# New due times, an opening set by hand and one multiplication on GpSimd in a four-layer graph-attention kernel whose instruction order a planner writes

## The chip, the cores and the metric

The kernel runs on one core of a Trainium2 chip. The metric is device time in microseconds (us) of one execution. Seven executions of the kernel before took 2975.5 to 2980.1 us, with a median of 2978.17 us. One execution was recorded by the hardware profiler; all rows, groups, waits and timelines below come from it.

The engines are named as in the profile: PE is TensorE (matrix products), PEld its weight load, DVE is VectorE, ACT is ScalarE, POOL is GpSimd, and SP is SyncE, which here only issues transfers. ACT's queue (ACTq) can issue transfers too. "L582" is line 582 of the kernel's source.

## The reference

Sixteen entries of 1024 nodes by 256 features pass through four graph-attention layers, each with a layer norm and a ReLU in front and a residual behind. All entries share one 1024 by 1024 mask, `adj`.

```python
# layer 0 (four heads of 64); layer 3 is the same with another a
h = jnp.maximum(_layernorm(x), 0.0)
Wh = (h @ W).reshape(B, N, 4, 64)
e = s_src[:, :, None, :] + s_dst[:, None, :, :]      # scores: Wh times the vectors a
e = jnp.where(e > 0, e, 0.2 * e)
alpha = softmax(where(mask, e, -inf), axis=2)
x = x + elu(einsum('bijh,bjhd->bihd', alpha, Wh))
# layer 1: one head of 256, scores of the same form
# layer 2: e = (h @ W1) @ (h @ W2).T, values h @ W3, relu in place of elu
```

## The kernel before

**Tiles.** A node set is cut into eight tiles of 128 nodes, and the mask and the attention weights into two halves of 512 query nodes. One weight tile `p` is 128 key nodes by 512 queries. Layers 0 and 3 make 64 such tiles for each entry (two halves, four heads, eight key tiles), layers 1 and 2 make 16 each.

**A layer's steps.** Statistics of x on DVE (L822 and L823). Then the norm's factors in three steps: `norm` (L855, DVE), `norm2` (L858, a power on POOL) and `norm3` (L861, DVE, which gives `nshift`). ACT makes the normed h (L891). h is turned over, either on PE (L906, then the copy L929) or, for nearly all entries, by a transposing DMA from SP (L918, with copies L914 and L932). PE projects it onto W and the score columns (`projected`, through the helper at L582). `evict` (L968 to L977, ACT) takes the exponentials of the scores: `ke` for the factors and the last column of `val`; in some layers `scaled` (L983, DVE) then multiplies the values by that column. The factors are spread to rows of 512: for entry 0 of layer 0 and entry 15 of layer 3 by PE and ACT (L1025 and L1029), otherwise through DRAM (L1047, L1051, L1064). `weigh` makes a weight tile with one DVE instruction (L1117 in layers 0 and 3, L1208 in layer 1). Layer 2 makes its scores on PE, exponentials on ACT (L1235, L1236) and cuts them with two DVE instructions (L1240, L1241). `attend` multiplies the weights with `val` on PE: into `acc` in layers 0 and 3, into `accb` in layers 1 and 2. Last come a reciprocal (L1150 or L1267), a division (L1164 or L1161 into `o`, L1273 or L1275 into `o1`), the ELU (L1083, L1084, L1088) and the addition to x: on DVE (L1090) or, in the layers that are marked `filling` (layer 0, and layer 3 of the last two entries), on POOL (L1097).

**The opening.** SP issues three transfers for x of entry 0 (L636), four quarters of the mask (L729), and then the later weights. ACT issues `w0` (L654) and its vector `a` (L664) and then loads its table with a first exponential (`warm`, L715). The score columns of `w0` are made by scaling `a` (L674), multiplying (L684) and adding up (L697), all on DVE, in two chunks c = 0 and 1. Each mask quarter is compared on DVE (`pos`, L737), turned over on PE (L595) and kept by a copy (L750: DVE for the first half, ACT for the second).

**What sets the order.** `Plan` (L79 on) takes every step with an engine, a cost in us, a due time, the steps it comes after, and the buffers it takes and gives. It plays these forward in the build, always taking the ready step with the earliest due, and writes the instructions in the order found. Nothing of costs and dues remains in the program but this order. At run time an engine waits only on semaphores that follow from data and buffers; a step that is planned "after" another without sharing data with it is kept back only by its place in its queue.

Due times come from tables: `PERIOD` (190 us for an entry), `START` and `LATER` (where a layer of an entry starts), `LEAD`, `AHEAD` and `STEP` (how far ahead its prologue lies, and the spacing in it), `WHEN` (steps of layers 1 and 2) and `EARLY` (how much earlier the ends are due). `SOON` is a due before all others. Buffers of note: eight for `p` (layers 0 and 3), eighteen for `p1`, two for `acc`, one for `o`, four for `pp` (the shared accumulator banks).

Of the kernel before, what the change touches and what calls it, by code (L numbers as in the profile page):

```python
# [45 lines left out]

PERIOD, EARLY = 190.0, 0.7407
START = {0: 0.0, 1: 1.0372, 2: 2.297, 3: 3.5524}  # L50
LEAD = {0: 0.7046, 1: 0.4612, 2: 0.2956, 3: 1.6786}
STEP = {0: 0.01, 1: 0.0686, 2: 0.0892, 3: 0.0445}
WHEN = {
    (1, "weights"): ((-0.5242, 0.0026), (-0.1464, 0.0419)),
    (1, "attended"): ((0.7567, 0.0147), (0.2574, 0.106)),
    (2, "weights"): ((-0.0331, 0.0103), (0.3531, 0.0135)),
    (2, "attended"): ((0.642, 0.0926), (0.4636, 0.0079)),
# [3 lines left out]
    (1, 0): 0.596, (1, 1): 0.958, (13, 2): 0.03, (13, 3): 0.392, (14, 3): -0.089, (0, 2): -0.137, (12, 2): 0.2,  # L61
    (13, 1): -0.61, (13, 0): 0.042, (0, 1): 0.165, (14, 2): 0.012, (12, 3): 0.381, (15, 2): 0.061,
    (14, 1): 0.153, (0, 3): -0.204, (0, 0): 0.005, (15, 1): 0.169, (3, 0): -0.106, (3, 2): -0.226,
    (3, 1): -0.037, (3, 3): 0.253, (14, 0): -0.403, (15, 3): 0.422, (12, 0): 0.216, (2, 2): -0.002,
    (2, 3): -0.052, (12, 1): -0.053, (1, 3): 0.022,
}
AHEAD = {
    (1, 0): 0.818, (15, 3): 0.338, (12, 1): 1.914, (15, 1): 0.404, (1, 3): -1.162, (0, 3): 0.168,
    (14, 2): 0.163, (14, 1): -0.3, (1, 1): -0.058, (0, 2): 0.142, (13, 1): 0.271, (3, 1): 0.197, (14, 3): 0.426,
    (3, 3): -0.404, (2, 2): 1.115, (15, 0): -0.042, (12, 0): 0.12, (1, 2): 0.321, (2, 3): -0.168,  # L70
    (3, 2): -0.354, (2, 1): -0.221, (13, 3): -0.364, (0, 1): 0.057, (12, 3): 0.014, (0, 0): -0.016,
    (13, 2): -0.254,
# [467 lines left out]
def fast(  # L540
# [16 lines left out]
    nc = tc.nc  # L557
# [87 lines left out]
    def weight(w, name, due, a=None, heads=0, own=1):  # L645
# [10 lines left out]
        s = landed(plan.add(engine, 0.5, due, load), due, 256)  # L656
# [12 lines left out]
        s2 = landed(plan.add(engine, 0.5, due, load_a, take=("p1",)), due, own * d)  # L669
# [8 lines left out]
        for c in range(KC):  # L678

            def columns(c=c):  # L680
                wa = tiles["wa", c] = buf("u", [P, heads, 2, d], name="wa")
                for side in range(2):
                    of = tiles["a"][:, :, side, :]
                    (nc.vector if first else nc.gpsimd).tensor_mul(  # L684
# [7 lines left out]
            for hd in range(1 if first else heads):  # L692
# [15 lines left out]
                )  # L708
        return t, done[-1]

    first_x = load_x(0, SOON)

    def warm():

# [113 lines left out]
    class Layer:  # L828
# [7 lines left out]
        def prologue(self, due, step, stats, direct=False):  # L836
# [48 lines left out]
            for n, t0 in enumerate(range(0, NT, 2)):  # L885
# [37 lines left out]
                def kept(t0=t0):  # L923
# [4 lines left out]
                    if direct:  # L928
                        nc.scalar.copy(T["hT", t0], T["tp", t0])  # L929
                        return  # L930
# [544 lines left out]
```

## Time and profile before

The profiled execution took 2980.87 us on the device, of which the instructions span 2979.0 us.

| | PE | DVE | ACT | POOL |
|---|---|---|---|---|
| busy, us | 2914.0 | 2645.3 | 1922.6 | 234.5 |
| share of the span | 98% | 89% | 65% | 8% |

| group | count | busy, us | what it is |
|---|---|---|---|
| PE L582 acc<-val,p | 32768 | 1074.9 | attended values of layers 0 and 3 |
| PE L582 accb<-val,p | 8192 | 928.1 | attended values of layers 1 and 2 |
| PE L582 pp<-qT,hT | 2048 | 461.4 | scores of layer 2 |
| DVE L1117 p<-row,ke,mask | 2048 | 1460.2 | weights of layers 0 and 3 |
| DVE L1208 p<-row,ke,mask | 256 | 180.2 | weights of layer 1 |
| DVE L822 bn<-xt | 512 | 211.9 | statistics |
| POOL L1097 xt<-xt,o | 35 | 97.5 | additions to x on POOL |

A group's row gives line, engine, operation, output<-inputs and count, then busy time and mean ns of one. A timeline row gives start and duration in us, then the same names and a count (of merged instructions), and in brackets the idle time of that engine just before and what ended it. A row of the view by stretches gives, for each engine, the busy time and the number of instructions, then the granted PE clock (1.00 is full), the share of the 16 DMA engines that was busy, and GB/s. One product in the kernel's code can be two rows of the profile (the weights of one `p` give 16 rows of `acc`).

### The profile page before, as it was taken

The numbers are of one execution on the slowest core, as the hardware profiler recorded it, in microseconds if no ns is written. First come the engines' busy times: TensorE is split into PE (matmuls) and PEld (weight loads), VectorE is DVE, ScalarE is ACT, GpSimd is POOL, SyncE is SP. The second block draws the span as 40 slices with busy tenths as digits, with TensorE's granted clock in tenths as the row PEclk, the third lists the DMA queues.
The fourth block names the chain that finished last, engine by engine and source line by source line (L and its number), as shares of the span: only waits on it lengthen the run. The fifth ranks groups of instructions, "written<-read, shape, count | busy, mean of one in ns | idle before, by whom it ended". The sixth has DMA issues, their size and how long they took to land.

```text
span 2979.0 us, 108647 instructions
## 1 busy us (share of the span) xinstructions
PE 2914.0 (98%) x47954; PEld 2326.2 (78%) x47954; DVE 2645.3 (89%) x5286; ACT 1922.6 (65%) x4776; POOL 234.5 (8%) x151
## 2 busy tenths in 40 slices
PE   7799999999999999999999999999999999999997
PEld 5776868779697887878779787786877869796876
DVE  8989988899898899989899898988999999796698
ACT  6767776785656767566675656766656684656543
POOL 2111100000100000000000100000000010000001
PEclk9899999999999999999999999999999999999999
DMA  4432223332222332413233222231413332121210
GB/s 126 94 59 59 64 50 97 63 69 73 44 71 61 70 72 61 79 38 87 48 66 77 48 77 44 72 75 38 90 42 70 76 62 57 41 57 35 53 35 25
DMA packets 344049, 188.06 MB, mean 63 GB/s; under 512 B 268881, under 2 KB 304401, under 8 KB 343569
## 3 DMA queue, kind: packets, MB, share of 16 engines
q1 hardware_dynamic: 343152, 180.51, 27.0%
q8 instruction: 378, 6.19, 0.9%
q14 instruction: 103, 0.84, 0.1%
q10 hardware_dynamic: 416, 0.52, 0.1%
HBM read 98.63 MB, written 17.33 MB: 39 GB/s over the span
## 4 chain that ended last, share of the span: by engine, by line
PE 84%; DVE 13%; ACT 1%; issue 1%; DMA 0%; POOL 0%; SPq 0%; DVEq 0%; POOLq 0%
PE pp L582 31%; PE accb L582 27%; PE acc L582 26%; DVE p L1117 8%; DVE o L1088 1%; DVE bn L822 1%; DVE xt L1090 0%; DVE p L1241 0%; DVE mv L823 0%; DVE p L1240 0%; DMA xt<-in_x_dram 0%; ACT hTp L932 0%; POOL xt L1097 0%; DMA turned<-planes 0%; DVE rden L1150 0%
## 5 line engine op out<-in xcount | busy, mean ns | idle before, releaser
L1117 DVE SCALAR_TENSOR_TENSOR p<-row,ke,mask 128x512 f32<-128x512 f32 x2048 | 1460.2, 767 | 34.0 <-PE acc L582 32.7
L582 PEld LDWEIGHTS acc<-val,p 128*64 128x64 f32 x32768 | 1073.0, 139 | 121.0 <-issue 47.2
L582 PE MATMUL acc<-val,p 128*64 128x65 f32 x32768 | 1074.9, 223 | 38.9 <-DVE p L1117 33.8
L582 PE MATMUL accb<-val,p 128*64 128x257 f32 x8192 | 928.1, 380 | 0.0
L582 PEld LDWEIGHTS accb<-val,p 128*64 128x64 f32 x8192 | 736.0, 136 | 130.1 <-issue 4.1
L582 PE MATMUL pp<-qT,hT 128*64 128x512 f32 x2048 | 461.4, 592 | 0.0
L582 PE MATMUL pp<-w,hTp 128*64 128x264 f32 (+1 forms) x3072 | 382.9, 387 | 3.0 <-ACT hTp L932 2.0
L582 PEld LDWEIGHTS pp<-qT,hT 128*64 128x64 f32 x2048 | 171.4, 137 | 211.6 <-issue 209.0
L582 PEld LDWEIGHTS pp<-w,hTp 128*64 128x64 f32 x3072 | 245.1, 138 | 84.4 <-issue 14.1
L891 ACT ACTIVATE h<-xt,nshift,rstd 128x256 f32<-128x256 f32 x512 | 275.5, 596 | 38.3 <-DVE nshift L861 38.2
L1240 DVE SCALAR_TENSOR_TENSOR p<-u,p 128x512 f32<-128x512 f32 x256 | 175.7, 686 | 127.8 <-ACT p L1236 127.5
L1275 ACT ACTIVATE o<-accb,rdens 128x256 f32<-128x256 f32 x128 | 60.5, 473 | 347.3 <-DVE rdens L1267 340.8
L914 ACT COPY planes<-h 128x512 uint16<-128x512 uint16 x496 | 281.7, 621 | 0.0
L932 ACT COPY hTp<-turned 128x1024 uint16<-128x1024 uint16 x184 | 214.0, 1167 | 28.5 <-DMA turned<-planes 28.3
L822 DVE BATCH_NORM_STATS2 bn<-xt 128x6 f32<-128x256 f32 x512 | 211.9, 414 | 13.4 <-DMA xt<-in_x_dram 5.4
L1235 ACT ACTIVATE u<-pp 128x512 f32<-128x512 f32 x256 | 152.9, 597 | 104.7 <-PE pp L582 79.3
L1164 ACT ACTIVATE o<-acc,rden 128x64 f32<-128x64 f32 x572 | 132.2, 316 | 113.3 <-DVE rden L1150 99.8
L858 POOL TENSOR_TENSOR rstd<-rstd,neg_half 128x8 f32<-128x8 f32 (+2 forms) x67 | 124.5, 1858 | 975.9 <-DVE rstd L855 643.2
L1241 DVE TENSOR_TENSOR p<-p,mask 128x512 f32<-128x512 f32 x256 | 179.2, 700 | 8.8
L1097 POOL TENSOR_TENSOR xt<-xt,o 128x1024 f32<-128x1024 f32 x35 | 97.5, 2786 | 1131.7 <-DVE o L1088 980.3
L1208 DVE SCALAR_TENSOR_TENSOR p<-row,ke,mask 128x512 f32<-128x512 f32 x256 | 180.2, 738 | 0.5 <-DMA row<-er_d 0.5
L977 ACT ACTIVATE val<-pp,val 128x64 f32<-128x64 f32 (+1 forms) x640 | 179.5, 347 | 0.0
(87 smaller groups left out, 1911.9 us busy)
## 6 DMA issues: line engine op xcount, KB each, us to landing
row<-er_d SPq DMA_DIRECT2D x272, 256.0 KB, 3.4
xt<-in_x_dram SPq DMA_DIRECT2D x31, 512.0 KB, 5.2
out_dram<-xt SPq DMA_DIRECT2D x31, 512.0 KB, 3.6
raw<-in_adj_dram SPq DMA_DIRECT2D x4, 1024.0 KB, 15.3
raw<-in_adj_dram SPq DMA_DIRECT2D x16, 256.0 KB, 3.3
turned<-planes SPq DMA_TRANSPOSE x248, 3.1
xt<-in_x_dram SPq DMA_DIRECT2D x2, 256.0 KB
w<-in_L_gnn_W_dram SPq DMA_DIRECT2D x2, 256.0 KB
```

Source lines behind the costliest of these rows:

```text
L582: nc.tensor.matmul(to[c : c + COLS], stationary[:, c : c + COLS], moving, start=start, stop=stop, skip_group_check=True,)
L822: nc.vector.bn_stats(st, x_tiles[b][:, t, :])
L891: nc.scalar.activation(h, x_tiles[b][:, t, :], AF.Relu, bias=T["shift"][:, t : t + 1], scale=T["rstd"][:, t : t + 1],)
L914: nc.scalar.copy(to[:, :, :, k, :], of)
L932: nc.scalar.copy(bits, T["tp", t0].rearrange("p s c q -> p c q s"))
L977: nc.scalar.mul(to[:, hd, :], of[:, hd, :], a[:, hd, :])
L1117: nc.vector.scalar_tensor_tensor(p, lay.rows[half, hd], lay.ke[:, lay.heads + hd, jt : jt + 1], mask_of(half, jt), op0=OP.max, op1=OP.mult)
L1164: nc.scalar.mul(to[:, t, :], acc[:, t, :d], rden[:, t, :])
L1208: nc.vector.scalar_tensor_tensor(p, lay.rows[half, 0], lay.ke[:, 1, jt : jt + 1], mask_of(half, jt), op0=OP.max, op1=OP.mult)
L1235: nc.scalar.activation(u, e, AF.Exp, scale=1.0 - SLOPE)
L1240: nc.vector.scalar_tensor_tensor(p, u, 1.0, p, op0=OP.max, op1=OP.mult)
L1241: nc.vector.tensor_mul(p, p, mask_of(half, jt))
```

## The change

It has six parts.

1. **Tables.** `EARLY`, `START`, `LEAD`, `STEP`, `WHEN`, `LATER` and `AHEAD` have new values, so all entries are ordered anew.
2. **Dues in the opening.** x of entry 0 is due 10 us ahead of `SOON`, `warm` 9, `w0` 6, the mask's first quarter 5.2, its second 1.5, and the norms and the prologue 5. The statistics are spaced by 0.5 in place of 0.9, and the norm steps of all three parts are due together.
3. **Order of loads.** In the plan the mask's loads come after parts of x, and the loads of `w1`, `w2v`, `w3` and the two raw weights of layer 2 after the first mask quarter.
4. **`w0`'s score columns.** The multiplication of chunk c = 1 is issued on POOL in place of DVE and no longer waits for chunk 0.
5. **Rows.** A new list `factored` holds the `evict` steps. The spreading of rows, and the factors that go through DRAM, come after these, no longer after `scaled`. The first half's rows of the two PE-turned layers are due 2.5 steps earlier.
6. **Costs in the plan.** `norm2`, `pos`, `keep` and the multiplication have other cost entries. `TURNED_ON_PE` names the two layers that `direct` named, so the same two turn h on PE.

Both programs have the same instructions but for one: two of the multiplications at L684 are on POOL in place of DVE.

```diff
-PERIOD, EARLY = 190.0, 0.7407
-START = {0: 0.0, 1: 1.0372, 2: 2.297, 3: 3.5524}
-LEAD = {0: 0.7046, 1: 0.4612, 2: 0.2956, 3: 1.6786}
-STEP = {0: 0.01, 1: 0.0686, 2: 0.0892, 3: 0.0445}
+TURNED_ON_PE = ((0, 0), (15, 3))
+PERIOD, EARLY = 190.0, 0.8711
+START = {0: 0.0, 1: 1.0292, 2: 2.3297, 3: 3.7503}
+LEAD = {0: 0.5727, 1: 0.718, 2: 0.2478, 3: 2.1041}
+STEP = {0: 0.0094, 1: 0.0707, 2: 0.069, 3: 0.055}
...
-    (1, 0): 0.596, (1, 1): 0.958, (13, 2): 0.03, (13, 3): 0.392, (14, 3): -0.089, (0, 2): -0.137, (12, 2): 0.2,
...
-    (3, 1): -0.037, (3, 3): 0.253, (14, 0): -0.403, (15, 3): 0.422, (12, 0): 0.216, (2, 2): -0.002,
...
+    (1, 0): 0.176, (1, 1): 0.626, (13, 3): 0.356, (0, 2): -0.59, (12, 3): 0.485, (14, 1): 0.247, (0, 3): -0.2,
...
+    (14, 0): -0.416, (2, 2): -0.232, (2, 0): -0.016, (3, 0): -0.452, (15, 3): -0.422, (3, 3): 0.208,
...
-        s = landed(plan.add(engine, 0.5, due, load), due, 256)
+        begin = () if first else tuple(mask_ready[0, 0])
+        s = landed(plan.add(engine, 0.5, due, load, begin), due, 256)
...
-                    (nc.vector if first else nc.gpsimd).tensor_mul(
+                    (nc.vector if at_once else nc.gpsimd).tensor_mul(
...
-            m = plan.add(*((DVE, 0.7) if first else (POOL, 2.0)), due + 0.5, columns, (s, s2, *done), take=("u",))
+            m = plan.add(
+                *((DVE, 0.7) if first and c == 0 else (POOL, 1.7)), due + 0.5, columns, (s, s2, *(() if first else done)),
+                take=("u",),
+            )
...
-    first_x = load_x(0, SOON)
+    first_x = load_x(0, SOON - 10.0)
...
-    w0, w0_ready = weight(w_l0, "w0", SOON, a_l0, 4, 4)
-    plan.add(ACT, 1.6, SOON, warm)
+    plan.add(ACT, 1.6, SOON - 9.0, warm)
+    w0, w0_ready = weight(w_l0, "w0", SOON - 6.0, a_l0, 4, 4)
...
-            due, quarter = 15.0 + n if half else SOON + n, {}
+            due, quarter = 15.0 + n if half else -1.5 if jh else SOON - 5.2, {}
...
-            loaded = landed(plan.add(SP, 0.9, due, load, take=("x",)), due, 1024)
+            loaded = landed(plan.add(SP, 0.9, due, load, (first_x[2 if n == 0 else -1],), take=("x",)), due, 1024)
...
-                at = due - (len(parts) - n - 1)
+                at = due - 5.0 * (len(parts) > 1)
                 s = plan.add(DVE, 0.2, at, norm, (*stats[its], ready[-1] if n else None))
-                s = plan.add(POOL, 2.0, at, norm2, (s,))
+                s = plan.add(POOL, 0.6 + 0.17 * (its.stop - its.start), at, norm2, (s,))
...
                     s2 = plan.add(ACT, cost, at, evict, (s2,), give=() if many else ("pp",))
+                    factored.append(s2)
...
-                            PE, 0.44, at + (half * heads + hd) * 0.01, spread, tuple(evicted[half * HT : (half + 1) * HT]),
+                            PE, 0.44, at - 2.5 * step * (1 - half) + (half * heads + hd) * 0.01, spread, tuple(factored[half * HT : (half + 1) * HT]),
...
-            due, step = SOON, 0.1
-            stats = [statistics(b, t, due - 2.5 + t // 2 * 0.9, (loads[b][t],)) for t in range(NT)]
+            due, step = SOON - 5.0, 0.1
+            stats = [statistics(b, t, due - 2.5 + t // 2 * 0.5, (loads[b][t],)) for t in range(NT)]
```

## The prediction

> **What bounds the kernel now.** First the slices of the span (40 of 74.5 us) and four stretches of it.
>
> ```profile
> PE   7799999999999999999999999999999999999997
> DVE  8989988899898899989899898988999999796698
> PEclk9899999999999999999999999999999999999999
> ```
>
> ```profile
> 0.00:75.00 75.00, 56.61 (x1040) 43.61 (x1040) 63.58 (x138) 46.46 (x141) 16.38 (x22) 1.00 0.43 127
> 75.00:200.00 125.00, 105.36 (x1986) 92.33 (x1988) 117.78 (x247) 84.37 (x256) 16.81 (x10) 0.89 0.36 74
> 200.00:2900.00 2700.00, 2689.36 (x43530) 2136.16 (x43528) 2399.37 (x4789) 1766.30 (x4303) 189.53 (x117) 1.00 0.28 62
> 2900.00:2979.00 79.00, 62.64 (x1404) 54.10 (x1400) 64.60 (x116) 25.43 (x77) 11.79 (x3) 0.91 0.07 23
> ```
>
> PE is idle for 65.0 us in all: 18.4 up to 75, 19.6 up to 200, 10.6 in the 2700 us that follow, and 16.4 in the tail. The middle is PE at work; a new order can win next to nothing there. In the first 200 us and the last 79, DVE is busy 94% and 82% of the time, and PE waits for it. The waits of PE say so by name:
>
> ```profile
> PE acc L582 <- DVE p L1117: 33.8, 34, 8.3
> PE pp L906 <- ACT h L891: 12.0, 1, 12.0
> PE acc L582 <- ACT o L1164: 3.9, 1, 3.9
> ```
>
> The timeline of the opening shows where DVE itself is late, and one later row what POOL does to it:
>
> ```profile
> 9.55 0.43 DVE L822 BATCH_NORM_STATS2 bn<-xt 128x6 f32<-128x256 f32 x1 [0.23 <-DMA xt<-in_x_dram]
> 11.16 0.13 DVE L861 SCALAR_TENSOR_TENSOR nshift<-mv,rstd 128x2 f32<-128x2 f32 x1
> 18.50 0.15 DVE L861 SCALAR_TENSOR_TENSOR nshift<-mv,rstd 128x4 f32<-128x4 f32 x1
> 19.30 5.25 PE L582 MATMUL pp<-w,hTp 128*64 128x264 f32 x28 [1.02 <-DVE w L697]
> 27.39 4.29 POOL L684 TENSOR_TENSOR wa<-w,a_bc 128x256 f32<-128x256 f32 x4 [11.57 <-DVE a_bc L674]
> 27.76 3.42 DVE L1117 SCALAR_TENSOR_TENSOR p<-row,ke,mask 128x512 f32<-128x512 f32 x3
> ...
> 70.70 2.81 POOL L1097 TENSOR_TENSOR xt<-xt,o 128x1024 f32<-128x1024 f32 x1 [6.47 <-DVE o L1088]
> 71.30 2.76 DVE L1117 SCALAR_TENSOR_TENSOR p<-row,ke,mask 128x512 f32<-128x512 f32 x1
> ```
>
> The first weight starts only at 27.76. A weight takes 0.667 us in a run (4.70 for 7 at 52.20); beside POOL's addition one took 2.76.
>
> **The method.** Both programs hold the same instructions, so I compare instruction orders. I price them by rows: a weight 0.667 on DVE, its product on PE 0.466 (3.73 for 128 rows); a statistics pair 0.53; an `accb` tile 3.48 (17.40 for five); a projection tile 0.88. For a weight, its lag is the DVE work listed up to and with it, less the PE work listed ahead of its product. PE's lost time there is at least that lag plus all that DVE waited or was slowed.
>
> **Opening and fill, before.** The lag is largest at a weight behind 160 weights, 56 statistics pairs and the rest: 106.7 + 29.7 + 11.5 (ELU) + 13.9 (mask, values) + 8.6 (small ones) = 170.4 of DVE. PE has 136.7 ahead: 143 products 66.7, eight `accb` tiles 27.8, 33 projections 29.0, turns 13.2. Lag 33.7. In the trace this product starts at 196.7, so 60.0 was lost, and DVE's own waits and slowdowns are 60.0 - 33.7 = 26.3. Of these, 11.6 lie before the end of the 7th weight (36.75 by the clock, 25.2 of work); 14.7 come after.
>
> **The opening, after.** SP's first twelve loads keep their order; "behind x" is only in the plan, since no wait was added between them. One SP load moves: the second raw weight goes ahead of x of entry 1. It took 0.43 to issue, and that x is first read at 39.48, 18 us after it was issued: nothing, or 0.43 without that cover. On ACT's queue the table load (1.28) and the exponential (0.20) now precede the two `w0` issues, which go from 0.74 to some 2.3. `w0` landed 3.8 after its issue, so 6.1; DVE scales `a` at about 12. Nothing, by that cover; without it, up to 1.6.
>
> On DVE, `nshift` of part 1 comes after the first statistic of part 3 in place of the fourth: 9.55 + 0.61 = 10.1 against 11.16. The third comes at about 14.1 against 18.50, because the scaling (0.4), one multiplication (0.74) and one sum (0.69) are all that is left ahead of it, and the mask's eight steps come behind. POOL's two multiplications (1.09 each, as in the 4.29 above) start at 13.4 and end by 15.6; the second sum follows one mask copy, at 16.7 to 17.4, against 19.26. Six projections of 0.88 then end at 22.7, three spreads and a copy (0.57) later the first row stands, since rows no longer wait for the scaled values: first weight at 24.1. Two comparisons (0.37), four mask copies (0.64) behind PE's turns, two values and six weights later the 7th weight ends at 33.5. Its DVE work is 23.3, so waits are 10.2, 1.4 fewer. If x comes 0.7 sooner, without `w0` beside it, this is 0.7 more; if the `a` vector is late by the 1.6 above, it is gone.
>
> A rule that speaks against moving work to POOL is in the Trainium skill, SBUF — State Buffer, section Who interferes with whom: GpSimd and VectorE share a port pair as an exclusive lock, and a two-input VectorE instruction is fully blocked while GpSimd reads. The row at 71.30 agrees (2.1 us lost). By the rule the third `nshift`, which has two inputs, could be held for 1.09, and the sum below would be 1.1 smaller. The comparison beside POOL at 27.43 took its usual 0.42, and `nshift` comes before or just after POOL starts, so I leave it out.
>
> **The fill, after.** The lag peaks at 32.1 (PE work 100.1) and at 29.6 (PE work 156.6: 166.9 products 77.8, eight `accb` tiles 27.8, 43 projections 37.8, turns 13.2; DVE 186.3). Later waits: I keep the 14.7, and 11.0 to the first place. To them I add 0.6, since `w1`'s two pairs on POOL now stand beside weights alone: four weights at 61.76 beside one pair took 1.0 too long, three at 27.76 beside two pairs 1.4. Lost at the first: 32.1 + 10.2 + 11.6 = 53.9; at the second: 29.6 + 10.2 + 15.3 = 55.1. The second decides: 60.0 - 55.1 = 4.9 gained. Bounds: 0, if DVE's waits grow by what the lag shrinks, to 9, if the later waits are as short as at the first place and x is 0.7 sooner (60.0 - 53.9 + 0.7 = 6.8) and the three waits of DVE for PE's `acc` at 87, 91 and 108 (2.9 in all) go by a third to two thirds.
>
> **The middle.** With eight `p` buffers a weight cannot start before the product eight back is done. Counting DVE and PE work from there, the worst place from 300 on has 0.8 to spare before and 0.7 after: nothing. Bounds: 5.6, PE's stalls on weights from 600 to 2400, gained, to the same lost again, twice.
>
> **The tail.** After the last `accb` tile 79 weights' products remain before, 88 after. DVE's list from the last `accb` reciprocal is 58.2 against 65.0 us: 6.8 more, while PE's work ahead of that tile is 5.9 less. Net 0.9 lost. In the tail one POOL addition met weights and held the only `o` buffer:
>
> ```profile
> 2924.60 7.49 POOL L1097 TENSOR_TENSOR xt<-xt,o 128x1024 f32<-128x1024 f32 x1 [15.17 <-DVE o L1088]
> 2933.11 5.82 PE L582 MATMUL acc<-val,p 128*64 128x65 f32 x112 [3.93 <-ACT o L1164]
> ```
>
> After the change nine weights in place of eight lie in that gap: 0.7 less idle. Together 0.2 lost; from 3.9 gained (POOL at its usual 2.8) to 6.8 lost (PE not sooner at that tile).
>
> **Sum.** -4.9 + 0 + 0.2 = -4.7. The profiled execution took 2980.9 (span 2979.0 and 1.9 around it), 2.7 above the median: 2976.2 by it, and 2973.5 by the median of 2978.2. I call 0.2%, 6 us, what a measurement of this kernel can tell from no change.
>
> **Rivals.** *More falls away*: the first place decides (6.1), and POOL's addition in the tail meets no weights (3.9): 2968. For it: the lag is small where most waits were; against it: both additions stand beside weights in the new list too. *The opening's gain is waited out*: weights come sooner, but `acc` and `p` buffers come free at PE's pace, so DVE waits longer in the fill; part 3 does nothing: 2977. For it: 2.9 us of such waits already; against it: the lag itself shrinks by 4.1. *Slower*: a weight late in the repeating middle. The spare there is 0.7; the longest such stall in the middle was 1.2, and with DVE or ACT late by that much at one place in each of some 13 repeats PE loses 15.6: 2978 - 4.7 + 15.6 = 2989. It decides against me once PE's waits from 300 to 2700 exceed 15 us, where the stretches before give 8.9. For it: every due is new; against it: both orders have the same spare.
>
> **Numbers.** The forecast, 2970 to 2976, has 0.45; a third of it is over 6 us faster. More falls away 0.27; waited out 0.13; slower 0.15 (0.13 beyond 6 us). Faster 0.15 + 0.27 = 0.42, same 0.30 + 0.13 + 0.02 = 0.45, slower 0.13. The range goes from below the faster rival, for its own error, to part of the slow one: 2964 to 2982.
>
> **What would show it.** First weight at 24 and the 7th done by 34; PE idle under 17 up to 75 and its waits for weights down by some 5; the first mask copy beside POOL's multiplications; 18 us idle or less in the tail. It is wrong if the first weight comes later than 26, if PE's idle time from 200 to 2900 differs from 10.6 by more than 5, or if the tail is longer by more than 2.

## The result and the profile after

The changed kernel takes 2973.69 us (median of 24 runs, 2970.51 to 2976.21); the kernel before took 2979.43 in the same comparison (60 runs). The ratio is 0.9982 with a 95% interval of 0.9977 to 0.9988: 5.4 us less by the ratio (3.6 to 6.9 by its interval) and 5.7 by the medians, just inside the 0.2% that the prediction called "no change". The profiled execution took 2973.73 with a span of 2971.9, against 2980.87 and 2979.0 before.

The slices and the four stretches of the changed kernel answer to those shown of before (columns of a stretch: its length, busy time of PE, PE's weight loads, DVE, ACT and POOL with their instructions, then granted clock, DMA share, GB/s):

```profile
PE   7899999999999999999999999999999999999997
DVE  8998988789989898998989989889999989687788
PEclk9899999999999999999999999999999999999999
```

```profile
0.00:75.00 75.00, 58.73 (x1048) 45.13 (x1050) 63.69 (x137) 46.18 (x134) 15.38 (x22) 1.00 0.47 143
75.00:200.00 125.00, 110.32 (x2082) 92.36 (x2079) 120.13 (x251) 93.65 (x289) 21.39 (x14) 0.93 0.33 70
200.00:2900.00 2700.00, 2691.60 (x43490) 2111.94 (x43485) 2397.32 (x4796) 1757.54 (x4285) 184.47 (x116) 1.00 0.28 62
2900.00:2972.00 72.00, 56.76 (x1348) 49.19 (x1346) 63.72 (x103) 23.00 (x69) 5.71 (x2) 0.93 0.08 25
```

PE's idle time fell from 18.4 to 16.3, from 19.6 to 14.7, from 10.6 to 8.4 and from 16.4 to 15.2: 10.4 less in all. The span fell by only 7.1: PE was busy for 3.4 us longer over the same instructions (2917.4 against 2914.0). Time at half clock does not explain this, since less of PE's busy time fell into it (31.7 against 37.0); what does was not found. So idle time alone does not give the gain, and I use another measure below. The granted clock of 75 to 200 rose from 0.89 to 0.93; this column turned out to matter more than the prediction allowed.

The waits of PE by name (total, times, longest):

```profile
PE acc L584 <- DVE p L1126: 28.1, 29, 2.1
PE pp L914 <- ACT h L899: 11.6, 2, 10.4
PE pp L584 <- ACT hTp L940: 4.5, 4, 2.2
```

Waits for weights fell from 33.8 to 28.1, the longest from 8.3 to 2.1, and the 3.9 for POOL's addition in the tail is gone. The wait for `hTp` is new: 4.5, of which 2.2 at one place.

The timeline of the opening (start, duration, engine, line, what it writes and reads, and in brackets the idle time before it):

```profile
9.00 0.43 DVE L829 BATCH_NORM_STATS2 bn<-xt 128x6 f32<-128x256 f32 x1 [2.87 <-DMA xt<-in_x_dram]
9.56 0.13 DVE L868 SCALAR_TENSOR_TENSOR nshift<-mv,rstd 128x2 f32<-128x2 f32 x1
13.30 0.15 DVE L868 SCALAR_TENSOR_TENSOR nshift<-mv,rstd 128x4 f32<-128x4 f32 x1
25.13 0.75 DVE L1126 SCALAR_TENSOR_TENSOR p<-row,ke,mask 128x512 f32<-128x512 f32 x1 [0.48 <-ACT row L1038]
30.24 4.72 DVE L1126 SCALAR_TENSOR_TENSOR p<-row,ke,mask 128x512 f32<-128x512 f32 x7
```

```profile
12.63 1.42 POOL L687 TENSOR_TENSOR wa<-w,a_bc 128x256 f32<-128x256 f32 x2
```

```profile
17.28 6.62 PE L584 MATMUL pp<-w,hTp 128*64 128x264 f32 x48
```

The order on DVE is the one foreseen: two `nshift` come early, the third at 13.30 in place of 18.50, and the projections start at 17.28 in place of 19.30. The first weight comes at 25.13 (27.76 before) and the 7th ends at 33.6 (36.8 before).

**Where the time came from.** I use one measure throughout: the loss of PE at an `accb` tile, which is the time at which the tile starts in the trace less the PE work listed ahead of it, at the full clock's prices. The table reads it where 210, 330, 500 and 2000 us of PE work lie ahead, at the last `accb` tile, and from there to the end. All work together is 2868.0, so the last two columns add up to the span less that. The rows below the first two are the experiments. Each row is one execution.

| kernel | first weight | 210 | 330 | 500 | 2000 | last `accb` | after it |
|---|---|---|---|---|---|---|---|
| before | 27.76 | 63.5 | 64.9 | 64.9 | 77.8 | 83.7 | 27.3 |
| changed | 25.13 | 56.1 | 60.6 | 60.6 | 72.2 | 77.2 | 26.7 |
| open_old_tables | 26.64 | 61.9 | 66.0 | 72.0 | 82.3 | 88.2 | 26.4 |
| tables_only | 25.66 | 56.5 | 59.6 | 59.7 | 71.3 | 75.6 | 27.0 |
| w0_first | 25.39 | 56.2 | 60.6 | 60.7 | 73.0 | 78.0 | 26.2 |
| mult_on_dve | 26.49 | 57.0 | 61.4 | 61.5 | 74.8 | 79.8 | 26.9 |
| before_warm (less the added work) | 25.71 | 61.3 | 62.8 | 62.8 | 75.5 | 81.4 | 26.9 |
| after_warm (less the added work) | 25.68 | 57.1 | 61.5 | 61.5 | 73.5 | 78.5 | 26.4 |
| more_early | 26.51 | 63.6 | 68.1 | 68.1 | 80.6 | 85.6 | 26.3 |
| more_late | 24.03 | 54.4 | 65.1 | 65.2 | 77.4 | 82.4 | 26.7 |
| copies_sooner | 24.24 | 53.1 | 55.5 | 55.6 | 67.4 | 72.4 | 26.1 |
| adds_tail_on_dve | 25.09 | 56.0 | 60.4 | 60.5 | 73.2 | 77.8 | 23.9 |
| loads_free | 24.86 | 53.7 | 56.8 | 56.9 | 68.6 | 73.5 | 26.4 |
| three | 25.67 | 54.7 | 57.1 | 57.2 | 69.7 | 74.3 | 24.2 |

From before to changed the fill gains 7.4, 3.1 of it is given back between 210 and 330, the rest of the middle gains 2.2 (18.8 against 16.6 from 330 to the last `accb`), and the tail 0.6: 7.1 in all, the difference of the spans.

The table also shows how far one profile can be trusted. adds_tail_on_dve, copies_sooner and more_late differ from the changed kernel only from 350 us on or later; up to 210 us of work all four have the same order on every engine. Yet they lose 56.0, 53.1, 54.4 and 56.1 there, and their first weights come at 25.09, 24.24, 24.03 and 25.13. So differences of up to 3.0 at 210, and of 1.1 in the first weight, need no cause in the order.

### The profile page after: what moved, and what is told of

The parts are those of the page before. It is cut to its first block, busy times and chain, and to the rows that moved or that the text cites. A ratio compares the mean times of both kernels' runs of the same rounds, so it can differ in the third digit from the quotient of the medians.

```text
span 2971.9 us, 108633 instructions
## 1 busy us (share of the span) xinstructions
PE 2917.4 (98%) x47954; PEld 2298.6 (77%) x47954; DVE 2644.9 (89%) x5284; ACT 1920.4 (65%) x4776; POOL 227.0 (8%) x153
## 4 chain that ended last, share of the span: by engine, by line
PE 85%; DVE 11%; ACT 2%; issue 1%; DMA 1%; POOL 0%; SPq 0%; DVEq 0%; POOLq 0%
PE pp L584 31%; PE acc L584 27%; PE accb L584 27%; DVE p L1126 7%; DVE bn L829 1%; DVE o L1097 1%; DMA turned<-planes 1%; DVE mv L830 0%; DVE p L1250 0%; DVE p L1249 0%; ACT h L899 0%; DVE xt L1099 0%; ACT planes L922 0%; ACT hTp L940 0%; DVE p L1217 0%
## 5 line engine op out<-in xcount | busy, mean ns | idle before, releaser
L1126 DVE SCALAR_TENSOR_TENSOR p<-row,ke,mask 128x512 f32<-128x512 f32 x2048 | 1456.6, 766 | 63.5 <-PE acc L584 62.8
L584 PE MATMUL acc<-val,p 128*64 128x65 f32 x32768 | 1073.6, 223 | 29.0 <-DVE p L1126 28.1
L584 PEld LDWEIGHTS accb<-val,p 128*64 128x64 f32 x8192 | 702.8, 136 | 163.6 <-issue 5.1
L584 PEld LDWEIGHTS pp<-w,hTp 128*64 128x64 f32 x3072 | 249.9, 138 | 87.3 <-issue 18.4
L1284 ACT ACTIVATE o<-accb,rdens 128x256 f32<-128x256 f32 x128 | 60.7, 474 | 345.8 <-DVE rdens L1276 333.6
L1245 ACT ACTIVATE p<-pp,shift_col 128x512 f32<-128x512 f32 x256 | 175.8, 687 | 0.0
```

The lines of the kernel that those rows point to most:

```text
L584: nc.tensor.matmul(to[c : c + COLS], stationary[:, c : c + COLS], moving, start=start, stop=stop, skip_group_check=True,)
L1126: nc.vector.scalar_tensor_tensor(p, lay.rows[half, hd], lay.ke[:, lay.heads + hd, jt : jt + 1], mask_of(half, jt), op0=OP.max, op1=OP.mult)
L1245: nc.scalar.activation(p, e, AF.Exp, bias=shift_col, scale=SLOPE)
```

## The experiments

Medians and ratios against the kernel before on the same chip; each profile is one execution.

| kernel | median us | before us | ratio | 95% interval |
|---|---|---|---|---|
| open_old_tables | 2984.39 | 2978.39 | 1.0018 | 1.0009 to 1.0027 |
| tables_only | 2974.80 | 2978.39 | 0.9988 | 0.9979 to 0.9997 |
| w0_first | 2973.80 | 2978.39 | 0.9983 | 0.9974 to 0.9992 |
| mult_on_dve | 2975.61 | 2978.39 | 0.9988 | 0.9979 to 0.9997 |
| before_warm | 2978.06 | 2979.65 | 0.9998 | 0.9989 to 1.0007 |
| after_warm | 2975.11 | 2979.65 | 0.9987 | 0.9978 to 0.9996 |
| more_early | 2981.71 | 2979.65 | 1.0009 | 0.9999 to 1.0018 |
| more_late | 2980.70 | 2979.65 | 1.0006 | 0.9997 to 1.0015 |
| copies_sooner | 2971.88 | 2979.44 | 0.9973 | 0.9963 to 0.9982 |
| adds_tail_on_dve | 2971.65 | 2979.44 | 0.9973 | 0.9963 to 0.9984 |
| loads_free | 2971.38 | 2979.44 | 0.9974 | 0.9962 to 0.9985 |
| three | 2967.72 | 2979.11 | 0.9961 | 0.9947 to 0.9975 |

**The two halves of the change.** First all edits of the code with the old tables of due times, then the old code with the new tables.

```diff
 # open_old_tables: the changed kernel, with
-PERIOD, EARLY = 190.0, 0.8711
+PERIOD, EARLY = 190.0, 0.7407
...
 # tables_only: the kernel before, with
-PERIOD, EARLY = 190.0, 0.7407
+PERIOD, EARLY = 190.0, 0.8711
...
```

> The changed kernel with the tables of before (PERIOD to AHEAD): all edits of the opening, the old order of the layers. Theory: the opening's edits and the tables' order are separate gains that add up. By the listed work the largest lag falls from 33.7 to 32.5, and the first weight comes at some 25.3, 2.5 sooner than before, as in the changed kernel; the end comes 1.2 + 2.6 = 3.8 sooner, 2975.6 (ratio 0.9987); the half clock at 190 to 201 of before stays. Rival 1, the tables bring it all: 2979 (1.000), DVE waiting longer for acc after the early weight. Rival 2, the opening brings it all: 2973.7 (0.998).

> The kernel before with the new tables alone: the old opening, the new order of the layers. Theory: first weight at 27.8 as before; lag 32.9 at PE work 108 and 30.4 at 151; at the product where the changed kernel had lost 56.1 it has lost 56.1 + 2.6 + 0.8 = 59.5, 0.9 under the 60.4 of before, and it is free of the half clock at 190 to 201 (3.4 more), but stalls near 376 as the changed kernel does (3.2 back); tail 0.5 sooner: 2979.4 - 1.6 = 2977.8 (0.9995). Rival 1, the tables bring it all: 2973.7 (0.998). Rival 2, the opening brings it all and the new tables nothing: 2979.4 (1.000).

Both expectations missed by their medians, in opposite directions. The edits with the old tables are slower than before, by 0.18%; the tables with the old code are faster, by 0.12%, two thirds of what the whole change gives. The interval of tables_only (0.9979 to 0.9997) holds its expected 0.9995 as well as the 0.9982 of the whole change, and its profile loses 102.6 in all against 103.9 of the changed kernel, so the rival that the tables bring it all is not excluded. The halves do not add up (0.18% lost and 0.12% gained against 0.18% gained). The loss table shows why the first is slow: the fill is 1.6 better than before, which one order alone can show, and from 210 to 500 it loses 10.1 where before lost 1.4. The largest of the new stalls, in PE's timeline of open_old_tables:

```profile
528.59 6.68 PE L585 MATMUL accb<-val,p 128*64 128x257 f32 x44 [2.15 <-DVE p L1251]
```

It lies far behind the opening. The edits also change a price that the planner uses for every layer (POOL's `rstd` step from 2.0 to 0.6 plus 0.17 a tile) and those of the mask's steps (from 0.45 to 0.36 and 0.65), so they reorder the whole program. That the tables have to fit these prices is my reading; that this order stalls is shown.

The second surprise is the first weight of tables_only: 25.66, although its DVE order up to there is that of before. Its PE and DVE timelines:

```profile
19.12 3.34 PE L581 MATMUL pp<-w,hTp 128*64 128x264 f32 x28 [1.02 <-DVE w L696]
```

```profile
25.66 3.42 DVE L1116 SCALAR_TENSOR_TENSOR p<-row,ke,mask 128x512 f32<-128x512 f32 x3
```

The same 28 matmuls that took 5.25 at 19.30 in the kernel before take 3.34 here. In the profile of before PE still ran at half its clock then: the trace grants the full clock from 23.2 on, here from 18.4, in the changed kernel from 19.5. (The column prints 1.00 for the time ahead of its first record, so one has to look at the matmuls themselves.) So in the profile of before some 2 us of the first weight's 27.76 are the clock at the start. The changed kernel's profile lost time to it as well: its 48 projection matmuls took 6.62, and 5.56 in copies_sooner, which has the same order up to there and its full clock from 16.4. In copies_sooner's timeline x was read at nearly the same time as in tables_only (9.26 and 9.37), and the clock was early in both:

```profile
9.26 0.43 DVE L829 BATCH_NORM_STATS2 bn<-xt 128x6 f32<-128x256 f32 x1 [2.73 <-DMA xt<-in_x_dram]
24.24 0.75 DVE L1127 SCALAR_TENSOR_TENSOR p<-row,ke,mask 128x512 f32<-128x512 f32 x1 [0.48 <-ACT row L1039]
```

Compared in this way the change brings the first weight 1.4 forward (24.24 against 25.66) and the 7th 2.0 (32.7 against 34.7). Of the 2.6 by which the profiles of before and after differ, about half is the change.

**Parts of the opening alone.** w0_first puts ACT's first four instructions back into the old order; mult_on_dve gives the second multiplication back to DVE.

```diff
 # w0_first
-    plan.add(ACT, 1.6, SOON - 9.0, warm)
+    plan.add(ACT, 1.6, SOON - 5.5, warm)
 # mult_on_dve
-                    (nc.vector if at_once else nc.gpsimd).tensor_mul(
+                    (nc.vector if first else nc.gpsimd).tensor_mul(
```

> The changed kernel with ACT's first four instructions in the old order: the loads of w0 and the attention vector ahead of the table load and the exponential; every other queue is the same. Theory: these loads share the DMA engines with x of entry 0; the statistics of part 2 start at about 8.15 as before (4.97 after the change), but the chain to the first weight goes through part 3, which landed 0.55 later before: first weight at 25.7 instead of 25.1, end 0.5 later, 2974.2. Rival 1, the early x is what moved the first weight: part 2 at 8.15 and first weight at 27 or later, end near 2976. Rival 2, x came sooner for another reason: part 2 stays at 4.97 and nothing moves.

> The changed kernel with the second multiplication of the first layer's weight columns on DVE again (two instructions, 0.75 together), ahead of the third nshift; nothing else moves. Theory: nshift of part 3 at 14.0 instead of 13.30, first weight 0.3 to 0.7 later (25.5 to 25.8), lag at every later product 0.75 more, end 0.5 to 0.8 later: 2974.4. Rival, the pair on POOL held DVE up or came too late for the second sum: first weight not later than 25.1 and the end the same or up to 1 sooner.

DVE's timelines, first of w0_first, then of mult_on_dve:

```profile
8.20 0.43 DVE L829 BATCH_NORM_STATS2 bn<-xt 128x6 f32<-128x256 f32 x1 [2.51 <-DMA xt<-in_x_dram]
9.62 0.43 DVE L829 BATCH_NORM_STATS2 bn<-xt 128x6 f32<-128x256 f32 x1 [0.25 <-DMA xt<-in_x_dram]
25.39 0.75 DVE L1126 SCALAR_TENSOR_TENSOR p<-row,ke,mask 128x512 f32<-128x512 f32 x1 [0.48 <-ACT row L1038]
```

```profile
11.03 0.43 DVE L829 BATCH_NORM_STATS2 bn<-xt 128x6 f32<-128x256 f32 x1 [4.86 <-DMA xt<-in_x_dram]
15.99 0.16 DVE L868 SCALAR_TENSOR_TENSOR nshift<-mv,rstd 128x4 f32<-128x4 f32 x1
```

With the old order on ACT the second part of x lands at 8.20 again instead of by 4.97, and little else moves: first weight 0.3 later, median 0.1 later. This fits the theory that the part that counts is the third, and the first rival (first weight at 27 or later) is out; 0.1 in the median is too little to tell the theory from no effect at all. And here is a catch that one profile could not show. With the new order that third part was read at 9.00, 10.88, 11.03, 9.09, 10.84, 8.86, 9.26, 9.09, 9.87 and 10.49 in ten profiles; with the old one at 9.55, 9.37, 9.62 and 9.48 in four. So moving `w0`'s loads behind the exponential brings the second part forward by 3, which nothing needs, and makes the third, which the first weight waits for, come anywhere between half a microsecond sooner and one and a half later.

In mult_on_dve the third part came at 11.03, late by that. From its reading to the third `nshift` it takes 4.96, and 4.30 in the changed kernel: the pair costs its 0.66 there, close to the 0.75 expected. At 210 the loss is 0.9 higher, which is within what the same order shows from one execution to the next. The median is 1.9 higher, with overlapping intervals: the sign fits, its size is not resolved.

**The clock at the start.** Both kernels with PE kept busy before x arrives.

```diff
         nc.scalar.activation(faults[:, 0:1], ones, AF.Exp)
+        busy = buf("acc", [P, HALF])
+        for _ in range(44):
+            nc.tensor.transpose(busy[:, :P], ident, ident)
```

> The kernel before with 44 extra transposes of the identity on PE from 1.6 us on, into an accumulator that nobody reads, so that PE is busy while it would wait for x. Theory: the first weight of before was late because PE worked at half its clock up to 23 (28 projection matmuls took 5.25 at 19.30; with the tables alone, where the clock was full from 18.4, the same 28 took 3.34 at 19.12 and the first weight came at 25.66). With PE kept busy the projections take 3.3, the first weight comes at 25.7 instead of 27.76, and the end up to 2 sooner: 2977.4 by the profile's chance, about 2978 if other executions had less of it (ratio 0.9993 to 1.000). Rival, the first weight waits for DVE and ACT alone: first weight at 27.7, 2979.4.

> The changed kernel with the same 44 extra transposes. Theory: its first 48 projection matmuls took 6.62, 5.3 at full clock; first weight at 23.8 to 24.1 if x lands as before, end 1.1 sooner: 2972.6 (0.9977). Rival 1, the clock was full already where it matters: nothing, 2973.7. Rival 2, the extra work holds the first real transposes up: first weight later than 25.2, end up to 1 later.

PE's timelines, one row of before_warm and three of after_warm:

```profile
19.17 3.34 PE L582 MATMUL pp<-w,hTp 128*64 128x264 f32 x28 [1.26 <-DVE w L697]
```

```profile
1.37 7.66 PE L724 MATMUL acc<-ident 128*128 128x128 f32 x44 [1.37 <-POOL neg_half L607]
10.46 0.93 PE L917 MATMUL pp<-ident,h 128*128 128x128 f32 x4 [1.43 <-ACT h L902]
17.36 7.08 PE L584 MATMUL pp<-w,hTp 128*64 128x264 f32 x48
```

In before_warm the 28 matmuls take 3.34 and the first weight comes at 25.71, as expected; the loss at 210 is 61.3 against 63.5. Yet its time is that of before (0.9998, 0.9989 to 1.0007). That would fit if other executions of before did not lose the 2 us of the profiled one, which was 2.7 above the median of the first seven and 1.4 above that of the sixty; no second execution of before was profiled, so this is not shown, and the interval leaves room for a part of the 2 us. In after_warm the added work ended at 9.0 and the first real transposes came at 10.46: PE idled there and behind them, was at half clock from 13.6 to 20.5, and the first weight came at 25.68. Nothing was gained; the median is 1.4 above the changed kernel's, with overlapping intervals. That is the outcome of rival 2, but not by its reason: the transposes came about when they do in the changed kernel (10.46 against 10.38), the clock later.

In before_warm, too, the clock fell back behind the added work, to half from 14.1 to 17.5, and was full again just ahead of the projections, no sooner than in copies_sooner (16.4) or more_late (17.4), which have no added work. So its early clock can't be put down to the transposes, and neither run kept PE at full clock up to the work that matters.

before_warm and tables_only have the same opening (first weight 25.71 and 25.66, 7th weight done at 34.8 and 34.7). What they differ by at 210, 61.3 against 56.5, is the order of the fill with the half clock that it met (10.2 us of it from 188 on in before_warm, none there in tables_only): 4.8, more than the 3.0 that one order can show.

**Does DVE's list decide?** 5.3 us of repeated weights, once ahead of the largest lag (the 40th weight, below), once far behind it (the 250th, in more_late).

```diff
+                weighed.append(p)
+                for _ in range(9 if len(weighed) == 40 else 1):
                     nc.vector.scalar_tensor_tensor(
```

> The changed kernel with the 40th weight of entry 0 computed nine times in place of once: 5.3 us more of DVE work ahead of the places where the lag is largest. Theory (DVE's listed work plus its waits sets PE's loss in the fill): the loss at the products from 100 to 157 grows by all of it, the end comes 5.3 later, 2979.0, or 7 with one more window at half clock. Rival, DVE's waits for acc and p swallow the most of it: under 2 later, 2975.

> The changed kernel with the 250th weight computed nine times: 5.3 us more of DVE work at some 300 us, behind the fill, where DVE's listed work is 15 or more below the largest lag. Theory (with eight p buffers DVE is at most some 0.7 to 4 us ahead of PE there, so a late weight stops PE at once): PE idle 2 to 5 at that place and a window of half clock (1.7) behind it, end 3 to 6.5 later, 2977 to 2980. Rival, the listed lag decides alone: nothing, 2973.7.

more_early loses 7.5 more at 210 in its profile, of which 1.4 can be put down to its first weight, which was late because x was; against mult_on_dve, where x came as late, it loses 6.6 more. By the ratios it is 0.27% over the changed kernel (1.0009 against 0.9982), some 8 us, with intervals that leave room for 5.3 to 7. All of the added work reached the end, and the rival (under 2) is out. more_late shows that the same holds behind the fill: from 210 to 330 it loses 10.7 against 4.5. The windows at that place:

```profile
355.00:360.00 5.00, 1.44 (x30) 1.30 (x32) 4.83 (x10) 0.00 (x0) 0.00 (x0) 0.87 0.00 0
360.00:365.00 5.00, 5.00 (x99) 4.14 (x97) 5.00 (x9) 2.29 (x10) 0.00 (x0) 0.79 0.15 49
```

PE stands still for 3.6 of five microseconds and is then busy for five at a clock of 0.79. By the expectation's count the listed lag is lower there by 15 or more, but DVE could not use that, as the theory with its eight `p` buffers says. PE waited 3.22 and 1.42 for the late weights, and the 3.41 us at half clock cost another 1.7: together 6.3, about the 6.2 by which this stretch lost more.

**Where 3 us were given back.** PE's timeline of the changed kernel, and windows around it:

```profile
371.01 3.96 PE L584 MATMUL acc<-val,p 128*64 128x65 f32 x128
377.20 5.47 PE L584 MATMUL pp<-w,hTp 128*64 128x264 f32 x32 [2.24 <-ACT hTp L940]
```

```profile
375.00:380.00 5.00, 2.79 (x16) 1.70 (x18) 4.86 (x13) 4.94 (x13) 1.18 (x1) 0.79 0.14 27
380.00:385.00 5.00, 5.00 (x42) 3.12 (x40) 4.87 (x10) 4.59 (x20) 2.70 (x4) 0.87 0.16 32
```

ACT is busy throughout; the copy that PE waits for stands behind an `o` and two `ex` of another layer in ACT's queue. Two copies are taken forward, with nothing else moved:

```diff
+    for what, ahead_of in ((("kept", 4, 0, 0), ("normed", 4, 0, 6)), (("kept", 4, 0, 2), ("split", 4, 0, 4))):
+        fn, other = (plan.steps[placed[k]][3] for k in (what, ahead_of))
+        fns.remove(fn)
+        fns.insert(fns.index(other), fn)
```

> The changed kernel with two copies of ACT taken out of their places near 375 us: hTp of tokens 0 to 255 of entry 4, layer 0, goes ahead of the last normalisation pair of that layer, and hTp of the next 256 ahead of the planes copy that stood before it; nothing else moves on any engine. Theory: the changed kernel gave 4 back there, 2.24 in which PE waited for this copy, and 1.7 because PE then ran a stretch of 3.4 us at half clock; without the wait both go: PE loss at PE work 330 is 56.6 instead of 60.6, and, as PE is the bound from there on, the end comes 3.5 to 4 sooner, 2970 (0.9970). Rival, the wait moves to the next thing that is late (DVE's list or the planes behind): loss at 330 still 59 or more, end within 1 of 2973.7.

```profile
371.71 2.00 PE L584 MATMUL pp<-w,hTp 128*64 128x264 f32 x16
374.55 2.00 PE L584 MATMUL pp<-w,hTp 128*64 128x264 f32 x16 [0.84 <-ACT hTp L940]
```

In copies_sooner's timeline the wait is 0.84 instead of 2.24 and the clock stays full; the loss from 210 to 330 is 2.4 instead of 4.5. The theory's 4 was too much by half, since the second copy is still late. By the ratios the time falls by some 2.7 against the changed kernel (0.9973 against 0.9982), by the medians 1.8, with overlapping intervals. The profile's own 5.4 is more than that: this execution also had its full clock early (from 16.4), and its first weight 0.9 sooner.

**The tail.** The three wide additions of layer 3 of the last two entries go to DVE:

```diff
-                s = plan.add(POOL, 2.7, due, lambda: nc.gpsimd.tensor_add(xs(), xs(), T["o", key]), (s,), give=gives)
+                s = plan.add(POOL, 2.7, due, lambda: (nc.vector if self.layer else nc.gpsimd).tensor_add(xs(), xs(), T["o", key]), (s,), give=gives)
```

> The changed kernel with the three wide residual additions of layer 3 of the last two entries on DVE instead of POOL (its order on the other engines stays). Theory: beside POOL's addition one weight of DVE was held up by 2.1 at 2919 and again at 2944, and PE waited 3 each time; an addition of this size takes DVE 1.2 (28 of them in the middle, mean 1225 ns), so each place gets 0.9 shorter and the tail 1 to 2, or 3.5 if a half-clock stretch goes with it: 2972 (0.9976). Rival, DVE's list is what bounds the tail and the held-up weights were spare: 1.2 to 2.4 later, 2976.

The timelines near 2920, of the changed kernel and of adds_tail_on_dve:

```profile
2919.39 8.11 DVE L1126 SCALAR_TENSOR_TENSOR p<-row,ke,mask 128x512 f32<-128x512 f32 x9
2919.46 2.86 POOL L1106 TENSOR_TENSOR xt<-xt,o 128x1024 f32<-128x1024 f32 x1 [22.63 <-DVE o L1097]
...
2922.92 3.33 PE L584 MATMUL acc<-val,p 128*64 128x65 f32 x64 [2.07 <-DVE p L1126]
```

```profile
2920.60 1.21 DVE L1106 TENSOR_TENSOR xt<-xt,o 128x1024 f32<-128x1024 f32 x1
...
2921.73 5.38 DVE L1126 SCALAR_TENSOR_TENSOR p<-row,ke,mask 128x512 f32<-128x512 f32 x8
...
2922.52 2.67 PE L584 MATMUL acc<-val,p 128*64 128x65 f32 x64 [1.11 <-DVE p L1126]
```

Nine weights beside POOL's addition take 8.11, that is 2.1 more than nine of 0.667; the addition on DVE costs 1.21. PE's wait falls from 2.07 to 1.11, neither of the two places is followed by half clock any more, and the tail shrinks from 26.7 to 23.9. The theory holds in the trace, between its 2 and its 3.5: 2.8. The ratio agrees (some 2.7), with intervals that overlap.

**The loads.** The plan's conditions on loads are undone:

```diff
-        begin = () if first else tuple(mask_ready[0, 0])
+        begin = ()
...
-            loaded = landed(plan.add(SP, 0.9, due, load, (first_x[2 if n == 0 else -1],), take=("x",)), due, 1024)
+            loaded = landed(plan.add(SP, 0.9, due, load, take=("x",)), due, 1024)
...
-            loaded = landed(plan.add(SP, 0.5, due, load, tuple(mask_ready[0, 0]), take=("p1",)), due, 256)
+            loaded = landed(plan.add(SP, 0.5, due, load, take=("p1",)), due, 256)
```

> The changed kernel with the plan's conditions on loads undone (mask quarters no longer behind x of entry 0, later weights and raw weights no longer behind the first mask quarter). SP's first twelve loads keep their order; what moves is the scaling of w1's attention vector (two DVE instructions, 0.5, now ahead of the first weight), POOL's four multiplications for w1 and the order of some projections. Theory: this part of the change is worth next to nothing: first weight 0.5 later, listed lag 32.3 at 101 and 30.9 at 138 against 32.1 and 29.6, end 0.2 to 1 later, 2974.3. Rival, keeping POOL and ACT free of w1 while the first weights run is what the opening gained: end 3 or more later, 2977.

Not 0.2 to 1 slower but some 2.3 faster than the changed kernel. In its profile the fill loses 53.7 instead of 56.1, which is within what the changed order itself shows (53.1 to 56.1), and its stall near 376, as long as the changed kernel's, met no half clock, by the chance of its place (below). What moved: `w1`'s four multiplications stand together on POOL at 24.65, beside one weight (1.07 in place of 0.75) and mask steps, while the changed kernel has them in pairs at 44.70 and 59.44 beside weights. That this is a cause was not isolated, and the interval (0.9962 to 0.9985) reaches over 0.9982: that the conditions cost time is not shown, only that undoing them does not cost the 3 or more of the rival.

**All three together.**

> The changed kernel with three edits at once: the plan's conditions on loads undone, the two copies near 375 us sooner on ACT, and the three wide additions of layer 3 of the last two entries on DVE. Theory: the tail is a place of its own and adds its 2.2; the other two meet at the same place (the loads' run had a loss of 3.0 between PE work 210 and 330, the copies' run 2.4, the changed kernel 4.5), so the copies add some 1 to the loads' 2.3: 2973.7 - 2.2 - 2.3 - 1 = 2968.2 (0.9962). Rival 1, all three add up in full: 2967 or less (0.9957). Rival 2, the fill's gains were chance of the clock's phase and only the tail's remains: 2971.5 (0.9973).

2967.72, a ratio of 0.9961 (0.9947 to 0.9975): 0.5 from the theory. It is the fastest of the kernels here, 6 us under the changed kernel by the two ratios, and here the intervals do not overlap (0.9975 against 0.9977). Rival 1 (2967 or less) cannot be told from it. Rival 2 is not excluded by the interval, though the median speaks against it.

## Why the prediction was right, point by point

- **Sum.** It named 4.7 us, and 5.4 came by the ratio. The terms are less even than their sum. That the time, 2973.69, lies within 0.2 of the 2973.5 named is in part luck: the kernel before stood 1.3 higher in the comparison (2979.43 in place of 2978.17), and the terms below erred both ways.
- **What bounds it.** The reading holds: the gain came in the fill, where PE waits for DVE. One reading of a row is off: DVE's 94% is its share of 75 to 200; over the first 200 us it is 91% (63.58 + 117.78).
- **The opening, after.** The order foreseen on DVE is there, and its times fit to about a microsecond: projections at 17.28 (17.4), first weight at 25.13 (24.1), 7th weight done at 33.6 (33.5). The fit of the last is luck: the projections took 1.10 a tile at a late clock in place of 0.88, so the first weight was 1.0 late, and from there to the 7th it took 8.5 in place of 9.4. One sign is missing: the first mask copy (15.26) does not stand beside POOL's multiplications, which ended at 14.05, since the pair took 1.42, not twice 1.09. What failed is the term "1.4 fewer waits" as a property of the change. The first weight of before was late by 2 because of PE's clock in that execution, and the projection price of 0.88 was applied to the one side while the other ran at 1.5 a tile. With an early clock and x at 9.3 to 9.4 on both sides, the waits up to the 7th weight are 9.5 with the old opening (34.7 less 25.2 of work, tables_only) and 9.4 with the new one (32.7 less 23.3, copies_sooner): the 2.0 that the 7th weight gains is the shorter list. A late clock or a late x takes some or all of it back: first weight 25.13 and 25.09 with the clock full from 19.3 or later, 26.51 and 26.64 with x at 10.8 and 10.9 as well, against 25.66 and 25.71 of the old opening.
- **ACT's loads later: "nothing, by that cover".** The cover held for `w0` itself. The step left out what these loads do to the third part of x: with the new order its reading spreads over 8.9 to 11.0. The hoped-for 0.7 of x came to the wrong part.
- **Loads behind x: nothing.** SP's order was read rightly. Undoing the conditions made the median 2.3 us lower, which the intervals do not resolve. The plan orders POOL and DVE by them too; whether the 0.6 put down for `w1`'s pairs beside weights was too small is open.
- **The fill, after: 4.9 gained.** At the decisive products the loss fell from 60.0 to 56.1, 3.9, since the later waits were some 16.2 (56.1 less 29.6 and 10.3) in place of 15.3; by 210 us of work it fell by 7.4, since before ran another 10 us at half clock from 190 on and the new order does not. The order of the tables brings 4.8 of it (tables_only against before_warm). What the edits of the opening add is not resolved: 0.4 by the changed kernel's profile, 2.1 and 3.4 by more_late and copies_sooner, which have the same order up to there and an earlier clock. So the rival that the opening's gain is waited out in the fill is not excluded for the edits by themselves. The method, lag plus waits at the place of the largest lag, held: more_early moved the loss by all that was added. What it lacked is the clock.
- **The middle: 0.** Net 0.9 lost (3.1 given back near 376, 2.2 gained later); PE's idle time from 300 to 2700 is 8.2 against 8.9. The step counted only DVE's lead in `p` buffers, and the one stall that cost time, 2.24 and a half-clock step near 376, was a copy late on ACT. The spare of 0.7 and the price of the slower rival were about right in kind: more_late and open_old_tables are that rival, made on purpose and by accident.
- **The tail: 0.2 lost.** 0.6 gained. The term that was mis-sized is POOL's addition: it took its usual 2.86 and held a weight up, instead of being held up itself, at 7.49, as before.
- **The rule of the shared port.** The Trainium skill, SBUF — State Buffer, section Who interferes with whom, was weighed for the third `nshift`. It ran at 13.30 in its usual 0.15 while POOL's pair stood from 12.63 to 14.05, so the 1.1 that was left out did not come, and the trace does not show the rule there. At 2919 it does, one weight held up by 2.1, and taking the addition off POOL there was worth more than its 1.21 on DVE.

## What to carry to other kernels

Before explaining a first stage by its order, look at how long one and the same matmul took in both profiles: a clock that came 4.8 us later (23.2 against 18.4) made 2 us here that no edit had caused. Runs that share an order up to some point show what one profile can tell; here 3.0 us at 210 was no difference. Where a planner sets the order, an edit of its prices is an edit of the whole program, so test the edits and the tables apart, and try a move of two instructions by hand before a new plan. A stall of PE costs its length plus what the half clock behind it takes, so stalls of the fill and the tail can be worth more than their idle time says.

## What the runs showed of the hardware

The clock of PE in these traces changes in steps of 3.41 us and is either full or half. A step of full clock in which PE idled for more than 1.9 us was always followed by one at half, one with less than 1.6 never, and in between both occurred (89 steps followed by half over the fourteen profiles, the shortest idle time 1.62; the longest that was not followed by it, 1.89). A half step was followed by another unless PE idled less than some 0.8 in it. So one wait of 2.2 us costs 2.2, or 2.2 and 1.7 (half a step), by where it lies on that grid: the stall at 376 met half clock in the changed kernel and none in tables_only and loads_free, whose stalls were as long.

The Trainium skill, TensorE: Matmul & The Clock Gate, section What's actually happening, states a free-running window of 3413 ns. The steps of 3.41 agree with it. The same section gives an idle window as what brings the half clock, and the section Why this matters for your kernels warns of gaps over some 3 us; here 1.6 to 1.9 us within a step could be enough.

The start of the full clock lay between 16.4 and 23.2 us in the profiles without the extra transposes, which between the profiles of before and tables_only, with the same order of work up to there, moved the first weight by 2.1. In before_warm and after_warm the clock was full from 7.3 and 6.8 on, with nothing but the added transposes ahead of it, and half again from 14.1 and 13.6. That the clock at the start also makes part of the 5.7 us by which runs of one kernel differ is likely, and was not tested.
